# The first layer norm of the mixers, taken for whole sequences in the experts' preparation

## The chip, the cores and the metric

The kernel runs on one core of a Trainium2 chip. A core has five engines that run their own instruction streams and wait for each other by semaphores: TensorE (PE in the profile, with PEld for its weight loads), VectorE (DVE), ScalarE (ACT), GpSimd (POOL) and SyncE (SP), which here issues nearly all DMAs. The metric is the time of one execution on the device in microseconds, less being better. A profiled execution gives a span, from the first to the last instruction, and a trace of every instruction.

## What is computed

The input is 16 sequences of 512 tokens with 128 features, in float32. Two blocks follow one another, each of the form x + mixer(norm(x)) * silu(experts(norm(x))):

```python
xn = _layernorm(x)
s = _L0_attn_ref(xn, ...)        # four layers, see below
g = _silu(_L0_ffn_ref(xn, ...))  # 8 experts, 2 chosen for each token
x = x + s * g
xn = _layernorm(x)
s = _L1_attn_ref(xn, ...)        # windowed attention, 16 heads of 64
g = _silu(_L1_ffn_ref(xn, ...))  # 32 experts, 4 chosen, and a shared one
x = x + s * g

def _layer(x, p):                # one of the four layers of _L0_attn_ref
    x = x + _attention(_layernorm(x, ln1w, ln1b), aw, ab, pw, pb)
    h = _layernorm(x, ln2w, ln2b)
    return x + gelu(h @ fw + fb) @ mw + mb
```

The mixer's `_attention` has no scores. It makes q, k and v, turns each into quaternions (the value, its difference to the token before, a rolled copy, a cosine), multiplies them pointwise, applies a fixed spectral filter and projects. Tokens meet only in the difference to the token before. Each of the four layers has two norms over the features, so each sequence needs eight. The change concerns the first of these eight.

## The kernel before

Features lie on the 128 partitions and tokens along the free axis, so a whole sequence is a tile of 128x512 and half a sequence one of 128x256. The program has two stages. The first does the mixer, both sets of experts and the routing; the second is the windowed attention and the last sum, and the change does not touch it.

**Mixers.** Four mixer streams p = 0 to 3 run through the first stage (`mixer_stream`, L532): streams 0 and 2 take the even sequences, 1 and 3 the odd ones; streams 0 and 1 take the first half of a sequence (h0) and 2 and 3 the second (h1). A name such as `f4h1l0a` is sequence 4, second half, layer 0, first norm; `b` is the second norm. Each stream has its own PSUM bank (m0 to m3), its own tile `big` and its own tile `normed[p]` of 128x256. The layer (`mixer_layer`, L427) is written as a Python generator: each `yield` ends a step, and a layer has ten: two for the first norm, then qkv, the cosines, the quaternion products, filter and projection, two for the second norm, the Gelu part and the last product. Four layers and one step for the output make `STEPS_M` = 41 steps for a sequence.

**A norm** (`norm`, L176) subtracts no mean here, because the mixer's data are in a basis where the mean is one component. It squares on ACT (L185), sums over the partitions by products with a column on PE into `pv` (L189, 128 tokens at a time), copies with an epsilon on ACT into `ve` (L198), takes the power -1/2 on POOL into `rs` (L200), spreads that over the partitions by products on PE into `bc` (L203), and multiplies on DVE (L213 for the mixers, L211 for the experts' norms, which subtract the mean first and call their tiles sq and xs).

**Experts.** The expert work is one sequence of jobs, called the feed. `prep0` (L246) prepares a sequence for the first experts: it loads x, norms it, turns it into the mixers' basis (the product `pz` on PE, the copy to the tile `z` on ACT, L258), hands z to the mixers through `given[b]`, computes the router's logits `pl`, chooses experts and writes the gates to DRAM. `loop0` (L284) then runs the eight experts, in 16 chunks: products `pg` (L299) and `pu` (L301), Silu (L303), a product on DVE (L304), the summing product `acc` (L305). `prep1` (L380) and `loop1` (L395) do the same for the second experts (L405 to L419); prep1 needs both halves of the first block's output for its sequence. The preparation of the next job is interleaved with the loop of the present one. All preparations share one PSUM bank, "b", the loops have one bank each for pg, pu and acc, and the tiles tagged "h" (three buffers) serve both the chunks of the loops and the norms of the preparations.

**The order.** A loop at the end of the stage calls the streams in turn, stream p starting `LAG * p` turns late (LAG = 5), and after each call advances the feed by a rate worked out from `STEPS_M`, so that a pair of sequences in the mixers meets its share of expert steps (9 per sequence of loop0, 18 of loop1). This gives the program order. Mixer steps are given a priority 400 instructions ahead of their place; from priorities and its own estimate of times a scheduler then makes the fixed instruction order of each engine. The engines run their orders strictly in turn, so an instruction that waits holds up all behind it on its engine.

**The first norm** of layer 0 is done in `mixer_layer` like any other: each stream norms its half of z into `normed[p]`, and the products of q, k and v (L443) read it. The same tile takes the other seven norms of the stream.

Of the kernel before, what the change touches and what calls it, by code (L numbers as in the profile page):

```python
# [10 lines left out]
F32 = mybir.dt.float32  # L11
# [4 lines left out]
P = 128  # L16
NB = 16
S = 512
# [12 lines left out]

TWO_PI_BELOW = 6.283185

STEPS_M, STEPS_0, STEPS_1 = 41, 9, 18

LAG = 5

# [18 lines left out]
def recurrent_kernel(ctx: ExitStack, tc: tile.TileContext, a, out):  # L56
    nc = tc.nc

    const = ctx.enter_context(tc.tile_pool(name="const", bufs=1))
# [14 lines left out]
    for l in range(L):  # L74
        t = wl.tile([P, W_END, P], F32, tag="lw", name=f"lw{l}")
# [20 lines left out]
    filt = cst[:, C_G : C_G + S]  # L96
# [23 lines left out]
    nc.gpsimd.memset(quarter, 0.25)  # L120

    normed = [const.tile([P, T], F32, name=f"normed{p}") for p in range(4)]
    for t in normed:
        nc.gpsimd.memset(t, 1.0)

    def fold(l, pa, pc, pool):
# [49 lines left out]
    def norm(src, dst, sq, bank, name, xs=None, p="e"):  # L176


        if xs is not None:
            xc = bank(f"xc_{name}")  # L180
            nc.tensor.matmul(xc, lhsT=centre, rhs=src, start=True, stop=True)
            nc.scalar.activation(sq, xc, AF.Square)
            nc.scalar.copy(xs, xc)
        else:
            nc.scalar.activation(sq, src, AF.Square)  # L185
        pv = bank(f"pv_{name}")
        n = src.shape[-1] // P
        for k in range(n):
            nc.tensor.matmul(  # L189
                pv[:, k : k + 1],  # L190
                lhsT=sq[:, k * P : (k + 1) * P],
                rhs=mean_col if xs is not None else mean_col0,
                start=True,
                stop=True,
            )
        yield
        ve = small.tile([P, NBLK], F32, tag=f"ve{p}", name=f"ve_{name}", bufs=2)
        nc.scalar.activation(ve[:, :n], pv[:, :n], AF.Identity, bias=eps)  # L198
        rs = small.tile([P, NBLK], F32, tag=f"rs{p}", name=f"rs_{name}", bufs=2)
        nc.gpsimd.tensor_tensor(rs[:, :n], in0=ve[:, :n], in1=nhalf[:, :n], op=ALU.pow)  # L200
        bc = bank(f"bc_{name}")
        for k in range(n):
            nc.tensor.matmul(  # L203
                bc[:, k * P : (k + 1) * P],
                lhsT=rs[:, k : k + 1].to_broadcast([P, P]),
                rhs=ident,
                start=True,
                stop=True,
            )
        if xs is not None:  # L210
            nc.vector.tensor_mul(dst, bc[:, : n * P], xs)  # L211
        else:
            nc.vector.tensor_mul(dst[: P - 1], bc[: P - 1, : n * P], src[: P - 1])  # L213
        yield
# [8 lines left out]
    def top_k(mask, n, k, name):  # L223

        best = small.tile([P, NBLK, 8], F32, tag="best", name=f"best_{name}", bufs=2)
        hit = small.tile([P, NBLK, n + 8 - k], F32, tag=f"hit{n}", name=f"hit_{name}", bufs=1)
        for i in range(NBLK):
            nc.vector.max(out=best[:, i, :], in_=chosen[n][:, i, :n])
        nc.vector.memset(best[:, :, k:], LOW)
        for i in range(NBLK):  # L230
            nc.vector.match_replace(
                out=hit[:, i, :], in_to_replace=best[:, i, :], in_values=chosen[n][:, i, :], imm_value=HIT
            )
        nc.vector.tensor_scalar(mask, hit[:, :, :n], HIT, None, ALU.is_equal)

    def to_rows(gates, n, gd, pool, bank, name):

        pg = bank(f"pt_{name}")
        for k in range(NBLK):
            nc.tensor.transpose(pg[:n, k * P : (k + 1) * P], gates[:, k, :], ident)  # L240
        gt = pool.tile([n, S], F32, tag=f"gt{n}", name=f"gt_{name}", bufs=1)
        nc.scalar.copy(gt, pg[:n, :])
        nc.sync.dma_start(gd, gt)


    def prep0(b, pool, ps, given, kept):  # L246

        name = f"e{b}"
        x = pool.tile([P, S], F32, tag="x", name=f"x_{name}", bufs=2)
        nc.sync.dma_start(x, a["xT"][:, b * S : (b + 1) * S])  # L250
        xn = pool.tile([P, S], F32, tag="xn", name=f"xn_{name}", bufs=2)
        sq = pool.tile([P, S], F32, tag="h", name=f"sq_{name}", bufs=3)
        xs = pool.tile([P, S], F32, tag="h", name=f"xs_{name}", bufs=3)
        yield from norm(x, xn, sq, ps["b"], name, xs)
        pz = ps["b"](f"pz_{name}")
        nc.tensor.matmul(pz, lhsT=basis, rhs=xn, start=True, stop=True)
        z = pool.tile([P, S], F32, tag="z", name=f"z_{name}", bufs=4)
        nc.scalar.copy(z, pz)  # L258
        last = small.tile([P, L, 3], F32, tag="last", name=f"last_{name}", bufs=6)
        given[b] = [z, None, last]  # L260
        pl = ps["b"](f"pl_{name}")
        for k in range(NBLK):
            nc.tensor.matmul(
                pl[:, k * NE0 : (k + 1) * NE0], lhsT=xn[:, k * P : (k + 1) * P], rhs=rw0, start=True, stop=True
            )
        plv = pl[:, : NBLK * NE0].rearrange("p (k e) -> p k e", e=NE0)
        work = chosen[NE0][:, :, :NE0]
        nc.vector.tensor_copy(work, plv)
        sg = small.tile([P, NBLK, NE0], F32, tag="sg0", name=f"sg_{name}", bufs=1)
        nc.scalar.activation(sg, work, AF.Sigmoid)  # L270
        mask = small.tile([P, NBLK, NE0], F32, tag="mk0", name=f"mk_{name}", bufs=1)
        top_k(mask, NE0, K0, f"{name}tk")
        yield
        nc.vector.tensor_mul(sg, sg, mask)
        den = small.tile([P, NBLK], F32, tag="den", name=f"den_{name}")
        nc.vector.tensor_reduce(den, sg, axis=AX.X, op=ALU.add)
        nc.vector.tensor_scalar_add(den, den, 1e-10)
        nc.vector.reciprocal(den, den)
        nc.vector.tensor_tensor(sg, sg, den.unsqueeze(2).to_broadcast([P, NBLK, NE0]), op=ALU.mult)
        to_rows(sg, NE0, gd0[b], pool, ps["b"], name)  # L280
        yield
        kept[0, b] = xn
# [141 lines left out]
        yield  # L424


    def mixer_layer(l, s, big, A, filt, last, bank, pool, name, p):  # L427


        first, last = last  # L430
# [2 lines left out]

        qkv = big.rearrange("p (i c) t -> p i c t", c=4)

        sq, h, z = big[:, 1, :], normed[p], big[:, 0, :]
        yield from norm(s, h, sq, bank, f"{name}a", p=p)
        raw, steps, turns = qkv[:, :, 0, :], qkv[:, :, 1, :], qkv[:, :, 3, :]
        for at in (slice(0, 2), slice(2, 3)):
            pq = bank(f"pq{at.start}_{name}")[:, : (at.stop - at.start) * T]  # L440
# [11 lines left out]
        for i, n in ((0, 2), (2, 1)):  # L452
            at = slice(i, i + n)
# [55 lines left out]
            s1, in0=po, scalar=turned[:, l, 0:1], in1=s, op0=ALU.add, op1=ALU.add  # L509
        )  # L510
        yield
        yield from norm(s1, h, sq, bank, f"{name}b", p=p)
        hid = A
        for i in range(0, 4, 2):
# [17 lines left out]
    def mixer_stream(seqs, half, pool, bank, p, given, written):  # L532

        at = slice(half * T, (half + 1) * T)
        for b in seqs:
            name = f"f{b}h{half}"
            while b not in given:
                yield
            z, _, last = given[b]
            s = z[:, at]  # L540
            for l in range(L):
                big = pool.tile([P, 12, T], F32, tag=f"big{p}", name=f"big_{name}l{l}")
                A = pool.tile([P, 4, T], F32, tag=f"A{p}", name=f"A_{name}l{l}")
                s = yield from mixer_layer(
                    l, s, big, A, filt[:, at], (half == 0, last[:, l, :]), bank, pool, f"{name}l{l}", p
                )
            while given[b][1] is None:
                yield
            x = pool.tile([P, T], F32, tag=f"xe{p}", name=f"x_{name}", bufs=1)
            nc.sync.dma_start(x, a["xT"][:, b * S + half * T : b * S + (half + 1) * T])  # L550
            g0 = given[b][1][:, at]
            pn = bank(f"pn_{name}")[:, :T]
            nc.tensor.matmul(pn, lhsT=basis, rhs=s, start=True, stop=True)
            nc.vector.tensor_mul(g0, pn, g0)
            nc.gpsimd.tensor_add(x, x, g0)
            nc.sync.dma_start(x1[b][:, at], x)
            written[b] += 1
            yield

    with (  # L560
# [3 lines left out]
        def banks(tag, n=1, width=S):  # L564
            return lambda name: psum.tile([P, width], F32, tag=tag, name=name, bufs=n)

        ps = {t: banks(t, n) for t, n in (("b", 1), ("g", 1), ("u", 1), ("acc", 1))}
# [53 lines left out]
    for i in range(2):  # L621
        t = wl.tile([P, NCH // 2, B_END, P], F32, tag="lw", name=f"aw{i}")
# [18 lines left out]
    with (  # L641
# [3 lines left out]
        ps = {  # L645
            tag: (lambda name, tag=tag, n=n: psum.tile([P, S], F32, tag=tag, name=name, bufs=n))
            for tag, n in (("pa", 2), ("ps", 2), ("pt", 2), ("po", 1), ("acc", 1))
        }
# [298 lines left out]
```

## Time and profile before

| | |
|---|---|
| median of 3 timed runs | 4145.51 us (4137.9 to 4149.45) |
| profiled execution, its own time | 4143.72 us |
| its span | 4141.9 us |
| mean granted TensorE clock | 0.979 |
| PE, DVE busy over the span | 3884.2 us (94%), 3465.7 us (84%) |
| ACT, POOL busy over the span | 2503.8 us (60%), 1626.7 us (39%) |
| first product of the attention stage | 2936 us |

The page divides the span into 40 slices of some 103 us and prints the busy share of each in tenths, 9 being 90% or more:

```profile
PE   8899989999999999899999999898999999999999
DVE  5788898989989898999888998985677777777776
ACT  3556665566565566556656565552477766767776
POOL 1122232222222223222222222220477777777776
```

The first 28 or so slices are the first stage, and the change of pattern on POOL marks the attention. Busy time is a mean over stages with different limits, so what a change is worth has to be read in its own stage. Matmuls are pipelined, and a busy PE in this profile is not PE at its peak. "Idle before" in a group's row is the time the engine stood still just ahead of these instructions, followed by what ended it; idle time of an engine that is not the limit costs nothing.

### The profile page before, as it was taken

To read this page: it belongs to the slowest core of one execution; us is meant where nothing else is said; L and a number is where in the kernel's file an instruction comes from. 1 tells how busy PE (TensorE), PEld (TensorE's weight loads), DVE (VectorE), ACT (ScalarE), POOL (GpSimd) and SP (SyncE) were. 2 spreads that over 40 slices of the span, in tenths; PEclk is the share of its full clock that TensorE was granted. 3 is DMA by queue.
4 is the path that set the end of the run, shared out by engine and by line. 5 is a ranking of instruction groups with operands and counts; after the bars stand their busy time and mean duration, and the time that the engine had idled before them with its cause. 6 is when DMAs were issued, how large, how long until landed. Compare 5 with 4: busy or idle time off the path is not lost. (4 is left out here: it accounts for less than half of the span.)

```text
span 4141.9 us, 56811 instructions
## 1 busy us (share of the span) xinstructions
PE 3884.2 (94%) x16936; PEld 2340.9 (57%) x16936; DVE 3465.7 (84%) x8220; ACT 2503.8 (60%) x5572; POOL 1626.7 (39%) x1885
## 2 busy tenths in 40 slices
PE   8899989999999999899999999898999999999999
PEld 5556655565555556566655655554455555555555
DVE  5788898989989898999888998985677777777776
ACT  3556665566565566556656565552477766767776
POOL 1122232222222223222222222220477777777776
PEclk8999999999999999999999999998999999999999
DMA  3222323322332332333233233243200000000000
GB/s 106 76 85 86 95 67 106 118 89 92 110 102 86 111 112 81 100 113 102 79 109 115 75 111 100 90 124 116 78 11 19 14 19 14 11 19 14 16 6 6
DMA packets 205972, 308.96 MB, mean 75 GB/s; under 512 B 29664, under 2 KB 121952, under 8 KB 205536
## 3 DMA queue, kind: packets, MB, share of 16 engines
q1 hardware_dynamic: 205520, 304.28, 24.1%
q8 instruction: 135, 2.21, 0.2%
q14 instruction: 173, 1.42, 0.1%
q10 hardware_dynamic: 144, 1.05, 0.1%
HBM read 236.79 MB, written 18.09 MB: 62 GB/s over the span
## 5 line engine op out<-in xcount | busy, mean ns | idle before, releaser
L405 PE MATMUL pg_m<-xn_m,w_m 128*128 128x512 f32 x544 | 294.4, 624 | 47.8 <-DMA w_m<-in_ew 40.7
L409 ACT ACTIVATE h_m<-pg_m 128x512 f32<-128x512 f32 x272 | 162.3, 597 | 278.2 <-PE pg_m L405 189.4
L407 PE MATMUL pu_m<-xn_m,w_m 128*128 128x512 f32 x544 | 288.7, 613 | 10.1 <-DVE h_m L410 9.9
L419 PE MATMUL acc_m<-h_m,w_m 128*128 128x512 f32 x544 | 284.6, 607 | 6.4 <-DVE h_m L418 5.8
L305 PE MATMUL acc_e<-h_e,w_e 128*128 128x512 f32 x512 | 270.2, 610 | 20.6 <-DVE h_e L304 20.2
L299 PE MATMUL pg_e<-xn_e,w_e 128*128 128x512 f32 x512 | 273.1, 615 | 16.2 <-ACT h_e L303 13.8
L301 PE MATMUL pu_e<-xg_e,w_e 128*128 128x512 f32 x512 | 265.0, 599 | 0.0
L410 DVE TENSOR_TENSOR h_m<-pu_m,h_m 128x512 f32<-128x512 f32 x272 | 185.6, 682 | 92.8 <-PE pu_m L407 69.1
L520 ACT ACT_TABLE_LOAD x203 | 260.4, 1283 | 3.6
L303 ACT ACTIVATE h_e<-pg_e 128x512 f32<-128x512 f32 x256 | 152.6, 596 | 181.5 <-PE acc_e L305 108.8
L304 DVE TENSOR_TENSOR h_e<-pu_e,h_e 128x512 f32<-128x512 f32 x256 | 174.6, 682 | 72.0 <-PE pu_e L301 67.7
L673 POOL TENSOR_TENSOR t_q<-t_q,rtab 128x512 f32<-128x512 f32 x128 | 162.6, 1271 | 91.3 <-DMA g_a<-g 88.8
L418 DVE TENSOR_TENSOR h_m<-gb_m,h_m 128x512 f32<-128x512 f32 x256 | 182.6, 713 | 16.1 <-DMA gb_m<-gd 14.9
L301 PEld LDWEIGHTS pu_e<-xg_e,w_e 128*128 128x128 f32 x512 | 98.5, 193 | 123.6 <-issue 123.6
L405 PEld LDWEIGHTS pg_m<-xn_m,w_m 128*128 128x128 f32 x544 | 95.4, 193 | 124.1 <-issue 74.3
L674 POOL TENSOR_TENSOR q<-q,t_q 128x512 f32<-128x512 f32 x128 | 163.1, 1274 | 0.1
L673 POOL TENSOR_TENSOR t_k<-t_k,rtab 128x512 f32<-128x512 f32 x128 | 162.6, 1270 | 0.9 <-DVE t_k L671 0.9
L674 POOL TENSOR_TENSOR k<-k,t_k 128x512 f32<-128x512 f32 x128 | 162.6, 1270 | 0.2
L685 PE MATMUL pv<-wv,xn_a 128*128 128x512 f32 x256 | 143.6, 644 | 11.2 <-DVE q L672 11.1
L407 PEld LDWEIGHTS pu_m<-xn_m,w_m 128*128 128x128 f32 x544 | 100.5, 195 | 89.7 <-issue 52.8
L668 PE MATMUL pa_q<-xn_a,aw 128*128 128x512 f32 x256 | 144.9, 648 | 5.3 <-DMA xn_a<-xn 5.3
L419 PEld LDWEIGHTS acc_m<-h_m,w_m 128*128 128x128 f32 x544 | 99.6, 192 | 81.2 <-issue 46.0
(6272 smaller groups left out, 11195.6 us busy)
## 6 DMA issues: line engine op xcount, KB each, us to landing
gb_m<-gd SPq DMA_DIRECT2D x512, 128.0 KB
w_m<-in_ew SPq DMA_DIRECT2D x272, 192.0 KB
w_e<-in_ew SPq DMA_DIRECT2D x128, 384.0 KB
gb_e<-gd SPq DMA_DIRECT2D x128, 256.0 KB
x_e<-in_xT SPq DMA_DIRECT2D x16, 256.0 KB
x_m<-x SPq DMA_DIRECT2D x16, 256.0 KB
xn<-xn_m SPq DMA_DIRECT2D x16, 256.0 KB
g<-g_m SPq DMA_DIRECT2D x16, 256.0 KB
```

Of the source, the lines that this page charges most:

```text
L299: nc.tensor.matmul(pg, lhsT=w[:, c, :], rhs=xn, start=True, stop=True)
L301: nc.tensor.matmul(pu, lhsT=w[:, 2 + c, :], rhs=xg, start=True, stop=True)
L304: nc.vector.tensor_mul(h, pu, h)
L305: nc.tensor.matmul(acc, lhsT=w[:, 4 + c, :], rhs=h, start=(e == 0 and c == 0), stop=(e == NE0 - 1 and c == HID0 // P - 1),)
L405: nc.tensor.matmul(pg, lhsT=w[:, 0, :], rhs=xn, start=True, stop=True)
L407: nc.tensor.matmul(pu, lhsT=w[:, 1, :], rhs=xn, start=True, stop=True)
L410: nc.vector.tensor_mul(h, pu, h)
L418: nc.vector.tensor_mul(h, gb, h)
L419: nc.tensor.matmul(acc, lhsT=w[:, 2, :], rhs=h, start=(c == 0), stop=shared)
L520: nc.scalar.activation(hid[:, i : i + 2, :], pf.rearrange("p (j t) -> p j t", t=T), AF.Gelu)
L673: nc.gpsimd.tensor_mul(t, t, rtab[:, 2 * which + 1, :])
L674: nc.gpsimd.tensor_add(dst, dst, t)
```

## The change

The first norm of layer 0 is taken out of the mixers and done in `prep0`, right behind the copy to z and before `given[b]` is set. It is done once for the sequence of 512 tokens instead of twice for 256. Its result goes to one of four new tiles `arrived` of 128x512, chosen by the sequence's number modulo 4, which the products of q, k and v of layer 0 read in halves. The new Square writes to a tile `sz` with the tag "h", and the sums and spread rows go through bank "b". The mixers' layer 0 has two steps less, and `STEPS_M` becomes 39. The other seven norms stay.

```diff
-STEPS_M, STEPS_0, STEPS_1 = 41, 9, 18
+STEPS_M, STEPS_0, STEPS_1 = 39, 9, 18
...
     normed = [const.tile([P, T], F32, name=f"normed{p}") for p in range(4)]
-    for t in normed:
+
+    arrived = [const.tile([P, S], F32, name=f"arrived{i}") for i in range(4)]
+    for t in normed + arrived:
         nc.gpsimd.memset(t, 1.0)
...
         nc.scalar.copy(z, pz)
         last = small.tile([P, L, 3], F32, tag="last", name=f"last_{name}", bufs=6)
+        sq = pool.tile([P, S], F32, tag="h", name=f"sz_{name}", bufs=3)
+        yield from norm(z, arrived[b % 4], sq, ps["b"], f"{name}z")
         given[b] = [z, None, last]
...
-    def mixer_layer(l, s, big, A, filt, last, bank, pool, name, p):
+    def mixer_layer(l, s, h0, big, A, filt, last, bank, pool, name, p):
...
-        sq, h, z = big[:, 1, :], normed[p], big[:, 0, :]
-        yield from norm(s, h, sq, bank, f"{name}a", p=p)
+        sq, h, z = big[:, 1, :], h0, big[:, 0, :]
+        if l:
+            h = normed[p]
+            yield from norm(s, h, sq, bank, f"{name}a", p=p)
...
+        h = normed[p]
         yield from norm(s1, h, sq, bank, f"{name}b", p=p)
...
                 s = yield from mixer_layer(
-                    l, s, big, A, filt[:, at], (half == 0, last[:, l, :]), bank, pool, f"{name}l{l}", p
+                    l, s, arrived[b % 4][:, at], big, A, filt[:, at], (half == 0, last[:, l, :]), bank, pool, f"{name}l{l}", p
                 )
```

## The prediction

> **What bounds the kernel now.** I read the page's digit rows first, to cut the span, then busy time by stage. One execution takes 4141.9 us of span, 4143.72 us with what lies around it; the three timed runs have a median of 4145.51 us, 1.8 us more. I sum against 4143.7.
>
> The busy times by stage (start:end, length, then PE, PEld, DVE, ACT, POOL busy, TensorE clock, DMA share, GB/s), steady part, end of the first stage, attention stage:
>
> ```profile
> 100.00:2850.00 2750.00, 2544.98 (x9526) 1595.72 (x9525) 2434.14 (x4400) 1612.64 (x2669) 718.57 (x817) 0.98 0.32 97
> 2791.50:2936.00 144.50, 121.26 (x310) 57.78 (x310) 72.77 (x163) 39.39 (x63) 6.82 (x9) 0.89 0.39 118
> 2936.00:4142.00 1206.00, 1180.12 (x6912) 655.20 (x6912) 933.74 (x3600) 840.02 (x2817) 896.11 (x1040) 1.00 0.05 16
> ```
>
> The change touches nothing in the third row; its 1206 us stay. In the first, PE is busy 93%, DVE 89%, ACT 59%, POOL 26%: two engines near full, and no single wait to pull out. As a busy PE includes pipelined overlap, I also took its pace from the starts of matmuls: a 512-column pass follows the last after 0.43 us, 256 after 0.215, 128 or fewer after 0.11. By these pitches the first stage is 2531 us of PE work in 2936 us. Between 100 and 2850 us the starts lie 361 us wider than that: 85 us ended on ACT, 60 on DVE, 50 on POOL (all at the broadcast products bc), 63 on a DMA or DMA with ACT, 84 at no wait (mostly the clock of 0.98). So the stage is paced by PE in a fixed order with small hiccups, and the change can only shift the hiccups.
>
> The groups of ACT (line, operation, tiles | busy, mean ns | idle before, who ended it):
>
> ```profile
> L520 ACT ACT_TABLE_LOAD x201 | 257.9, 1283 | 3.6
> L303 ACT ACTIVATE h_e<-pg_e 128x512 f32<-128x512 f32 x251 | 149.6, 596 | 173.3 <-PE acc_e L305 108.8 <-PE pg_e L299 51.3 <-PE acc_m L419 4.9
> L303 ACT ACT_TABLE_LOAD x102 | 130.9, 1283 | 7.2 <-PE pv_e L189 3.5 <-PE pv_m L189 1.3 <-DVE xn_m L211 0.6
> L409 ACT ACT_TABLE_LOAD x99 | 127.0, 1283 | 5.5 <-PE pv_m L189 3.8
> ```
>
> Two things to see: most of ACT's big rows are table switches, and the expert's Silu waits 108.8 us for acc_e, that is for one of the three buffers "h" to come free.
>
> One removed norm in order of time (start, length, engine, line), the first half of sequence 4:
>
> ```profile
> 697.58 0.50 PE L189 MATMUL pv_f4h0l0a<-cst,big_f4h0l 128*128 128x1 f32 x4
> 698.27 0.26 ACT L198 ACTIVATE ve_f4h0l0a<-pv_f4h0l0a,eps 128x2 f32<-128x2 f32 x1
> ...
> 698.61 0.83 POOL L200 TENSOR_TENSOR rs_f4h0l0a<-ve_f4h0l0a,nhalf 128x2 f32<-128x2 f32 x1 [0.59 <-ACT ve_f4h0l0a L198]
> ...
> 702.33 0.61 PE L203 MATMUL bc_f4h0l0a<-cst,rs_f4h0l0a 128*128 128x128 f32 x4
> ...
> 703.81 0.41 DVE L213 TENSOR_TENSOR normed<-bc_f4h0l0a,z_e 127x256 f32<-127x256 f32 x1
> ```
>
> It takes 6.6 us from pv to the product's end, but PE does other work from 698.1 to 702.3: the chain is hidden behind experts.
>
> **The change part by part.**
>
> *Work.* Removed, 32 times: Square 0.416, ve 0.258, rs about 0.70, product 0.424 us. Added, 16 times at 512 columns, by the rows of the expert norm: Square 0.597, ve 0.258, rs 1.03, product 0.682. ACT 21.6 - 13.7 = -7.9 us, DVE 13.6 - 10.9 = -2.7, POOL 22.4 - 16.5 = -6. PE nothing: four passes more or less either way (16x8 pv and bc passes for 32x4). None of this is on PE, so I cost it at nothing.
>
> *PE's waits at the norm.* Ahead of the 32 removed bc the starts show 5.4 us of hiccup, ahead of their pv 2.1. The nearest row for what comes is the expert norm in the same preparation: 1.2 and 1.4 us for 16. **-5 us** (from -7.5, no new wait, to +5, if each new norm waits as the router's norm does: 5.6 + 2.4 us there).
>
> *Table loads.* The instruction order shows 476 loads before and 416 after (Gelu 203 to 175, expert Silu 105 to 85, router-expert Silu 100 to 91). At 1283 ns that is 77 us of ACT. The Trainium skill, ScalarE: Activation LUTs, "What ACT_TABLE_LOAD costs", counts a drain of about 1380 ns on top, 2.66 us a switch: 160 us. The trace disagrees: a load at 1713.64 us ended at 1714.92 and the Silu began at 1714.94. I take 1283. But ACT idles 41% of the stage, so only what reaches PE counts: 85 us over 476 loads is 0.18 us a load, times 60 is **-11 us**. Ends: 0 (none on the path) and -43 (half of all that ended on ACT).
>
> *The new Square's buffer.* sz is taken from the three "h" that the expert loop rotates through. Its hold, from Square to last pv, is 4.4 us in the mean for sq_e. What that costs is in no row; near it is the hold of sq_e and xs_e together, 12.5 us, in which PE's hiccups are 16.8% against 14.0% overall (0.35 us each); for the router norm 22.3% of 14 us (1.15 us). **+6 us** for 16; ends 0 and +35 (PE loses half of 16 x 4.4).
>
> *What is queued behind.* In the preparation the router's logits now come after the new norm, since all use the one PSUM bank "b": the chain grows by about 12.5 us, as long as the first norm. The gates are written 22 us or more before the loop that needs them (sequences 4 and 5 the closest), apart from sequence 0; so at nothing, and 16 x a few us if that lead were gone. On ACT, Silus queue behind the new Square and ve; on POOL the mixers' differences behind rs, which waited 60.6 us for ve_e in its ten waits. A norm issues no DMA; SP only sees the layer-0 swaps earlier. The first pair has no lead: z of sequence 1 is used 4 us after it is made. But in the new order the first products of sequence 1 stand at the same place in PE's queue (row 104 in both), and half 1 of sequence 0 comes before the weight folding instead of amid it: nothing. The memsets of arrived, 4 x some 0.6 us (a 256-column one is 0.31), end before POOL's first rs (22 us).
>
> *Fewer steps.* Mixers go from 41 to 39 turns, and expert steps per turn rise to match. PE work is unchanged, so at a full PE this is worth nothing in itself; it moves the end of the stage.
>
> *The end of the stage.* Rows of PE in order of time:
>
> ```profile
> 2791.52 1.06 PE L181 MATMUL xc_m<-x_m,cst 128*128 128x512 f32 x2
> ...
> 2801.73 1.92 PE L323 MATMUL pl_m<-rw,xn_m 128*128 128x32 f32 x8 [3.25 <-DVE xn_m L211]
> 2803.46 2.05 PE L405 MATMUL pg_m<-xn_m,w_m 128*128 128x512 f32 x2
> ...
> 2827.60 3.09 PE L419 MATMUL acc_m<-h_m,w_m 128*128 128x512 f32 x4 [0.26 <-DVE h_m L418]
> ...
> 2837.83 1.02 PE L419 MATMUL acc_m<-h_m,w_m 128*128 128x512 f32 x2
> 2843.86 2.08 PE L181 MATMUL xc_m<-x_m,cst 128*128 128x512 f32 x2 [5.00 <-DMA x_m<-x]
> ```
>
> From the norm of sequence 14 (2791.5) to attention (2936) are 144.5 us for 104.2 us of PE work: 40 lost, part of it behind sequence 15, whose mixer ended late (the 5.00 us). In the new order the last mixer ends 105 us of PE work ahead of attention instead of 83, and the norm of 14 begins with 95.7 left and no mixer beside it. Its chain to the first acc (36 us here) then holds 11.7 us of work: 24 lost, the 5.00 us gone, 5 lost at attention's first load as now, some 5 for the cold clock: 34. That is 130 us, plus 8.5 us more work ahead of it at 0.88: 140. **-5 us**, ends -10 and +8. The skill's TensorE: Matmul & The Clock Gate, "What's actually happening", speaks against this step: after an idle window of some 3.4 us the array runs at half clock until it has been busy as long. The trace agrees (pairs 1.7 to 1.8 us apart at 2803 to 2811, 0.86 later), so a bare chain is paid twice. By the rule alone two cold windows would lose about 2 x 3.4/2 = 3.4 us; I took 5.
>
> *The redrawn order.* The scheduler re-sorts everything. PE work between a mixer's pv and its bc has a median of 3.4 us before and 3.0 after (68 of 256 under 2.5, then 77 of 226); between an expert's pu and acc, and Gelu and pm, the same. I cost it at nothing, +-15.
>
> Sum: -5 - 11 + 6 - 5 = -15 us: 4143.7 to **4129**, against the median 4145.5 about **4130 us**, 0.37% less.
>
> **Rivals.** *ACT is the true pace* (for: table loads are its largest rows; against: 41% idle, 85 us of PE's hiccups in all). The -11 becomes -43: 4097 us. Chance 0.08.
>
> *The h ring.* Place: L303's wait for acc_e. A slot lent to sz stops one chunk in three just when the ring is the limit, and the norm now sits in the expert's own order, no longer in the mixers' preferred one. Price: 16 x 4.4 us, half lost, +35 for the +6: about 4159 us; all lost, +70: 4194. It decides from 1.3 us per preparation, where it eats the 21 us of gains. For: 108.8 us of waits at that place. Against: the present two borrowers cost 0.35 us. Chance 0.26.
>
> *It moves nothing*: the norm was hidden before, table loads go from idle time, the end of the stage comes out even: 4144 us. For: ACT's 41%, the hidden chain above. Against: the 5.00 us. Chance 0.14.
>
> That the change does not do what it says is excluded: the norms l0a are gone from the order and 16 of 512 columns stand in it.
>
> **The numbers.** Forecast 0.52, by itself 4110 to 4148. A measurement here tells 0.3% (12 us) from no change. Faster: 0.36 of the forecast and the first rival's 0.08, 0.44. Same: 0.15 of the forecast, 0.11 of the third and 0.02 of the ring, 0.28. Slower: 0.24 of the ring, the rest of the others, 0.28. The range runs from the first rival's time to 4172, a little beyond the ring's half price.
>
> **What would show it.** ACT's loads at 416 and its busy time down by 80 to 90 us; PE's busy time unchanged; PE's hiccups ended on ACT near 75 us and on POOL below 50; ahead of the last x_m no wait; a bare stretch of some 20 us on PE behind the norm of sequence 14. The ring is right if L303's wait for acc_e grows by 20 us or more and PE waits at sz's pv. I am wrong altogether if the steady stage from 100 to 2700 us differs by over 1% at the same work: then the new order's own waits decide.

## The result, and the profile after

| | before | changed |
|---|---|---|
| median, lowest to highest | 4146.33 us (4137.9 to 4149.45, 4 runs) | 4164.18 us (4159.08 to 4166.02, 4 runs) |
| profiled execution, its span | 4143.72, 4141.9 us | 4163.71, 4161.9 us |
| mean granted clock | 0.979 | 0.978 |
| ACT busy, instructions | 2503.8 us, 5572 | 2422.5 us, 5480 |

The changed kernel takes 1.0044 [1.0027, 1.0062] of the time before: some 18 us more, where 16 less were forecast. The direction is wrong. That the time lies in the forecast's range is luck: the range reached up to 4172 us for the sake of the h ring, which is not what happened (below).

The same stages of the changed kernel (columns as in the prediction's first view; the first product of attention is now 17 us later, at 2953 us):

```profile
100.00:2850.00 2750.00, 2535.24 (x9472) 1590.60 (x9470) 2415.58 (x4372) 1525.87 (x2566) 720.78 (x796) 0.97 0.32 96
2950.00:4162.00 1212.00, 1182.56 (x6912) 656.32 (x6912) 934.79 (x3600) 840.17 (x2817) 896.40 (x1040) 1.00 0.05 16
```

In the first row ACT has 87 us less to do and PE has done *less* in the same 2750 us, 9472 matmuls for 9526. Attention is as it was. Two shorter stretches show where PE falls behind; first before, then changed:

```profile
100.00:400.00 300.00, 277.37 (x1005) 168.75 (x1004) 247.79 (x440) 170.99 (x287) 74.78 (x84) 0.97 0.27 83
400.00:2500.00 2100.00, 1963.27 (x7433) 1237.03 (x7432) 1901.77 (x3437) 1268.50 (x2092) 563.81 (x640) 0.99 0.33 99
```

```profile
100.00:400.00 300.00, 284.08 (x1084) 178.52 (x1083) 261.94 (x463) 173.07 (x294) 79.83 (x87) 0.98 0.28 84
400.00:2500.00 2100.00, 1943.89 (x7327) 1225.79 (x7326) 1873.62 (x3378) 1174.44 (x1987) 568.76 (x627) 0.98 0.33 96
```

Up to 400 us the changed kernel is ahead: 1084 matmuls for 1005. From 400 to 2500 us it makes 7327 where before makes 7433, 1.4% less on a stage that PE paces.

Equal times hold unequal work. So I gave each matmul of a trace the pitch that the prediction found for its width, summed these pitches to "PE work", and asked how much longer than its PE work each stretch *of work* took. A "hiccup" is the time by which the next matmul starts later than the pitch. The first stage is 2531 us of PE work in both kernels. The time over that, in one profiled execution of each:

| PE work, us | 0 to 300 (start) | 300 to 2200 (steady) | 2200 to 2531 (end) |
|---|---|---|---|
| before | 74 us | 229 us | 93 us |
| changed | 54 us | 271 us | 90 us |
| difference | -20 | +42 | -3 |

These make nearly all of the 20 us between the two profiled executions. By what ended PE's hiccups in the steady part, the 42 us are spread: DMA, alone or with ACT, 56 to 71; POOL 34 to 44; no wait shown 52 to 62 (the granted clock over this part is 0.986 before and 0.981 changed); DVE 34 to 42; ACT 55 to 52. No single wait carries them. How a hiccup with two causes is sorted matters: by the one releaser that the profile names, ACT goes from 54 to 61 and DMA from 47 to 55. Only the spread is firm.

The groups of ACT that the prediction showed, now, between 100 and 2850 us (L527, L307 and L413 are its L520, L303 and L409):

```profile
L527 ACT ACT_TABLE_LOAD x173 | 222.0, 1283 | 3.1
L307 ACT ACTIVATE h_e<-pg_e 128x512 f32<-128x512 f32 x250 | 149.1, 596 | 204.8 <-PE acc_e L309 110.0 <-PE pg_e L303 71.2 <-PE acc_m L423 5.1
L413 ACT ACT_TABLE_LOAD x90 | 115.5, 1283 | 3.0 <-PE pv_e L191 1.3 <-PE pv_m L191 0.2
L307 ACT ACT_TABLE_LOAD x83 | 106.5, 1283 | 9.2 <-PE pv_e4z L191 3.2 <-PE pv_e L191 2.6 <-PE pv_m L191 1.3
```

The loads went as forecast. The wait for acc_e, where the h ring would show, stands at 110.0 us for 108.8. PE's waits in the same window moved at places that no edit touches, the second experts' among them (line, waited for: us in total, times, longest); before, then changed:

```profile
PE pg_m L405 <- DMA w_m<-in_ew: 39.0, 39, 3.9
PE pg_m L405 <- ACT h_m L409: 5.3, 8, 1.4
```

```profile
PE pg_m L409 <- DMA w_m<-in_ew: 41.2, 38, 3.2
PE pg_m L409 <- ACT h_m L413: 14.5, 13, 2.5
...
PE bc_e5z L205 <- POOL rs_e5z L202: 3.5, 1, 3.5
```

The new norm has one noticeable wait, the last row; it was once late, not sixteen times.

### The profile page after: what moved, and what is told of

Same layout as the page of the kernel before. It is cut to its first block, busy times and chain, and to the rows that moved or that the text cites. A ratio compares the mean times of both kernels' runs of the same rounds, so it can differ in the third digit from the quotient of the medians.

```text
span 4161.9 us, 56676 instructions
## 1 busy us (share of the span) xinstructions
PE 3887.7 (93%) x16936; PEld 2340.1 (56%) x16936; DVE 3457.6 (83%) x8204; ACT 2422.5 (58%) x5480; POOL 1634.9 (39%) x1873
## 5 line engine op out<-in xcount | busy, mean ns | idle before, releaser
L413 ACT ACTIVATE h_m<-pg_m 128x512 f32<-128x512 f32 x272 | 162.4, 597 | 328.7 <-PE pg_m L409 223.5
L409 PE MATMUL pg_m<-xn_m,w_m 128*128 128x512 f32 x544 | 296.3, 627 | 61.1 <-DMA w_m<-in_ew 44.2
L303 PE MATMUL pg_e<-xn_e,w_e 128*128 128x512 f32 x512 | 269.3, 608 | 17.0 <-ACT h_e L307 10.9
L307 ACT ACTIVATE h_e<-pg_e 128x512 f32<-128x512 f32 x256 | 152.7, 596 | 209.1 <-PE acc_e L309 110.0
L409 PEld LDWEIGHTS pg_m<-xn_m,w_m 128*128 128x128 f32 x544 | 95.6, 195 | 143.8 <-issue 78.8
```

Source lines behind the costliest of these rows:

```text
L303: nc.tensor.matmul(pg, lhsT=w[:, c, :], rhs=xn, start=True, stop=True)
L409: nc.tensor.matmul(pg, lhsT=w[:, 0, :], rhs=xn, start=True, stop=True)
```

## The experiments

Every ratio is to the kernel before, run on the same chip, with its 95% interval. "Steady" is the middle column of the table above, and "start" and "end" are its neighbours; each is from one profiled execution, which lay up to 13 us from its kernel's median. Steady compares with 229 before and 271 changed. In the expectations, the "order theory" says that any new instruction order costs, and the "place" or "move" theory that the norm costs by standing in the preparation.

### The ring, the steps, the order: one part at a time

**A buffer of its own for sz.**

```diff
-        sq = pool.tile([P, S], F32, tag="h", name=f"sz_{name}", bufs=3)
+        sq = pool.tile([P, S], F32, tag="sz", name=f"sz_{name}", bufs=1)
```

> The changed kernel, with the new Square's tile sz in a buffer of its own instead of one of the three h that the expert loops rotate through. The h ring theory: most of the 18 us comes back, about 4148 us, and PE's hiccups in the steady stage fall. The order theory (the scheduler's new order is what costs, whichever edit draws it): the time has no reason to return; 4140 to 4175, since this edit redraws the order once more (table loads 484 instead of 416).

4178.4 us, 1.0085 [1.0071, 1.0098]; steady 262. Freed from the ring, the kernel is slower still. ACT's row for the first experts' Silu:

```profile
L307 ACT ACTIVATE h_e<-pg_e 128x512 f32<-128x512 f32 x251 | 149.6, 596 | 174.0 <-PE acc_e L309 93.2 <-PE pg_e L303 71.2 <-PE acc_m L423 4.6
```

The wait for acc_e fell from 110.0 to 93.2 us and the time rose by 14. As this edit redraws the order too, the run alone can't exclude a small price of the ring. But in the changed kernel's trace sz is held for 2.9 us in the mean, 16 times, and PE's hiccups in these stretches are 2.6% of the time. The ring as the cause falls.

**The changed kernel with 41 steps**: two empty steps in layer 0 in place of the removed ones.

```diff
-STEPS_M, STEPS_0, STEPS_1 = 39, 9, 18
+STEPS_M, STEPS_0, STEPS_1 = 41, 9, 18
...
+        else:
+            yield
+            yield
```

> The changed kernel with two empty steps in layer 0 where the norm was, so that a sequence takes 41 turns of the mixers again and the expert steps per turn are those of before. If the shorter count of steps (39) is what costs, it returns to about 4146. If the bunching of the streams costs (two or three streams finish a sequence within 30 us of PE work of each other, instead of evenly spread), it stays at 4155 or more, because its streams end at 0, 78, 98 and 106 us of PE work for sequences 8 and 9 (before: 0, 34, 65, 104; changed: 0, 68, 97, 103).

4159.67 us, 1.0035 [1.0022, 1.0048]; steady 257.

**The kernel before with 39 steps**: all norms as before, but that of layer 0 ends no step.

```diff
-STEPS_M, STEPS_0, STEPS_1 = 41, 9, 18
+STEPS_M, STEPS_0, STEPS_1 = 39, 9, 18
...
-        yield from norm(s, h, sq, bank, f"{name}a", p=p)
+        for _ in norm(s, h, sq, bank, f"{name}a", p=p):
+            if l:
+                yield
```

> The kernel before with the norm left in the mixers, in halves, but without its two steps in layer 0, so 39 turns. Only the step count changes. If the step count costs: about 4164, as the changed kernel. If what costs is where the norm stands (bank b, h, the experts' order): about 4146. The order theory: anything from 4135 to 4170; its streams end at 0, 61, 100, 111 and it loads 507 tables.

4179.66 us, 1.009 [1.0077, 1.0103]; steady 270, and slower than any of the times expected. The step count alone, with the same instructions on every engine but the table loads, costs 0.9%; given back to the changed kernel, it brings about 4.5 us, hardly more than the intervals. So it is no fixed price of two steps. It is a new order, and a new order can cost more than the whole change.

**The changed kernel, mixers 500 ahead.**

```diff
-AHEAD = 400
+AHEAD = 500
```

> The changed kernel with the mixers' priority 500 instructions ahead instead of 400; the same instructions in another order. Its streams end evenly spread, at 0, 44, 74 and 97 us of PE work for sequences 8 and 9, like before. The bunching theory: 4146 or less. The theory that the norm's new place itself costs (h ring, bank b): about 4164 as the changed kernel. The last mixer ends 152 us of PE work ahead of the attention (changed kernel: 105), which can cost some us at the stage's end under either.

4164.54 us, 1.0054 [1.004, 1.0068]; steady 260. The streams end evenly spread and nothing came back, so the bunching theory falls.

### Both kernels at other settings of the order

If any redrawing costs time, the kernel before must lose too when only the settings change. LAG is the delay between streams, AHEAD the mixers' priority; each edit is one number. First LAG 4 and AHEAD 300, in both kernels:

> The kernel before with LAG 4 instead of 5: the same instructions in another order, norm in the mixers. The order theory: before's own order is the odd one, so this is slower too, by 10 to 40 us (4153 to 4185). The theory that the norm's move itself costs in the steady stage: within some us of before, 4135 to 4155.

> The changed kernel with LAG 4. Its pair is e5. The order theory: as e5 or, by the start that became 15 to 20 us shorter with the norm in the preparation, 5 to 20 us below e5. The move theory: 15 to 20 us above e5. By the distances in PE's order alone (pv to bc under 2.5 us for 20% of the norms, 34% in the changed kernel) it would be the better of the changed orders: 4145 to 4155.

> The kernel before with the mixers' priority 300 instructions ahead. Again the same instructions in another order; its streams end bunched, at 0, 87, 123 and 125 us of PE work. The order theory: 4153 to 4185. The bunching theory: slow, 4160 or more. The move theory: 4135 to 4155.

> The changed kernel with 300 instructions ahead, the pair of e7; bunched as well (0, 84, 113, 122). The order theory: at e7 or up to 20 us below it. The move theory: 15 to 20 us above e7.

Then LAG 6 in both, and AHEAD 500 in the kernel before:

> The kernel before with LAG 6: the third neighbouring setting of it. If its setting of 5 and 400 is a chosen low point, 10 to 40 us above it (4152 to 4182), as LAG 4 (4172.6) was. Its streams end evenly spread (0, 22, 56, 95).

> The changed kernel with LAG 6, pair of e9. If the change by itself gains (20 us in the first 300 us of PE work, in every changed kernel so far but e1) and only the steady stage is redrawn, it ends below e9 as with LAG 4 (-18) and 300 ahead (-102). If the norm in the preparation costs in the steady stage by itself (+31 at LAG 4, +42 at LAG 5), it ends 10 to 25 above e9.

> The kernel before with 500 instructions ahead; the order changes little (streams end at 0, 40, 63, 103; table loads 497). Within 10 us of before (4135 to 4155) if nearness of the order is what keeps the time. Its pair is e4 (4164.5).

| LAG, AHEAD | before | changed | changed less before, from the ratios | from the profiles: start, steady, end |
|---|---|---|---|---|
| 5, 400 | 4146.33 us, 1 | 4164.18 us, 1.0044 [1.0027, 1.0062] | +18 us | -20, +42, -3 |
| 4, 400 | 4172.61 us, 1.0080 [1.0065, 1.0095] | 4154.49 us, 1.0037 [1.0024, 1.0049] | -18 us | -38, +32, -28 |
| 5, 500 | 4161.78 us, 1.0045 [1.0029, 1.0061] | 4164.54 us, 1.0054 [1.0040, 1.0068] | +4 us | -5, +15, -9 |
| 6, 400 | 4181.69 us, 1.0083 [1.0068, 1.0099] | 4191.82 us, 1.0116 [1.0099, 1.0132] | +14 us | -7, +55, -19 |
| 5, 300 | 4276.34 us, 1.0326 [1.0310, 1.0342] | 4174.72 us, 1.0088 [1.0072, 1.0103] | -99 us | -25, -47, -21 |

The left column holds the same work five times: 4146 to 4276 us, the present setting its lowest point. The changed kernel spans 4154 to 4192, and its best is elsewhere, at LAG 4. The sign of the change depends on the setting. An edit that redraws the order can give up a setting that was the best of its own family.

The last column shows more than scatter. At all five settings the changed kernel gains at the start and at the end, and at four of them it loses in the steady part. Nor does every redrawing cost in the steady part: the kernel before with LAG 4 is better there than with LAG 5 (214 for 229) and loses at the start (92 for 74) and at the end (134 for 93).

Three expectations missed here. The kernel before with 500 ahead was to stay within 10 us and took some 19 more; with 300 ahead it was to stay within 4185 us; and the changed kernel with 300 ahead was to end at most 20 us below that, and ended 99 below. That a near order keeps the time falls with the first.

The settings show something of the table loads too. The pages' first rows (busy us, share, instructions) of the kernel before with AHEAD 300, then of the changed one with LAG 4:

```profile
PE 3914.1 (92%) x16936; PEld 2344.4 (55%) x16936; DVE 3467.8 (81%) x8220; ACT 2457.7 (58%) x5538; POOL 1626.3 (38%) x1885
```

```profile
PE 3878.2 (93%) x16936; PEld 2343.4 (56%) x16936; DVE 3464.7 (83%) x8204; ACT 2494.3 (60%) x5539; POOL 1652.9 (40%) x1873
```

ACT's instructions other than loads are 5572 - 476 = 5096 before and 5480 - 416 = 5064 changed. So the slowest kernel here has only 442 loads, 34 fewer than the original, and the changed one at its best has 475, 59 more than at the present setting. The 60 loads saved belong to one order, not to the change, and the time doesn't follow their number.

### The size, the place and the shape of the moved norm

**Moved for sequences 0 and 1 only.** The others are normed in the mixers as before; 41 steps.

```diff
-        sq = pool.tile([P, S], F32, tag="h", name=f"sz_{name}", bufs=3)
-        yield from norm(z, arrived[b % 4], sq, ps["b"], f"{name}z")
+        if b < 2:
+            sq = pool.tile([P, S], F32, tag="h", name=f"sz_{name}", bufs=3)
+            yield from norm(z, arrived[b], sq, ps["b"], f"{name}z")
...
```

> The norm taken in the preparation for sequences 0 and 1 alone, 41 steps for all; the others norm in the mixers as before. The start's gain of 20 us should appear whole, so at 300 us of PE work the loss is near 62 us (before: 83). If the steady stage costs because the norm stands in the preparation, its steady loss is as before (229) and the time is about 4125. If any redrawn order costs there, 250 to 275 and the time is 4140 to 4170.

4143.89 us, 0.9995 [0.9985, 1.0005]. Its profiled execution was 10 us above its median, so its split (59, 255, 91) says only that the start was short again. Whether the start can be gained alone was tried once more, with AHEAD 450:

> The kernel of e12 (norm moved for sequences 0 and 1 only) with 450 instructions ahead. The start's gain of 15 us stays; the steady loss is a new draw, 215 to 275 by what the others showed: 4125 to 4170, most likely 4150.

4178.09 us, 1.0074 [1.0058, 1.009], start 75. The gain at the start was expected to stay and did not: moving the norm of the first pair alone does not secure it.

**The moved norm four times over**, with its two steps ended only behind the last.

```diff
-        sq = pool.tile([P, S], F32, tag="h", name=f"sz_{name}", bufs=3)
-        yield from norm(z, arrived[b % 4], sq, ps["b"], f"{name}z")
+        for i in range(4):
+            sq = pool.tile([P, S], F32, tag="h", name=f"sz{i}_{name}", bufs=3)
+            for _ in norm(z, arrived[b % 4], sq, ps["b"], f"{name}z{i}"):
+                pass
+        yield
+        yield
```

> The changed kernel with the moved norm done four times over in the preparation (the result of the last is used). PE gets 3 x 16 x 1.75 = 84 us more work. The order theory: 4164 + 84, +-25, so 4223 to 4273. The place theory (each norm in the preparation costs some 40/16 = 2.5 us of hiccups in the steady stage beyond its own work): 3 x 42 more, so 4360 or above.

4238.3 us, 1.0223 [1.0202, 1.0244]: 74 us over the changed kernel for 83 us more PE work (2614 for 2531 by the same pitches). Forty-eight more of these norms, each with its Square, its hold of the ring and its place in bank "b", cost no more than their passes on PE, as far as one draw of the order can tell. No hidden price shows that grows with the number of norms.

**The moved norm with the mixers' priority.**

```diff
-        sq = pool.tile([P, S], F32, tag="h", name=f"sz_{name}", bufs=3)
-        yield from norm(z, arrived[b % 4], sq, ps["b"], f"{name}z")
+        with tc.high_priority(offset=AHEAD):
+            sq = pool.tile([P, S], F32, tag="h", name=f"sz_{name}", bufs=3)
+            for _ in norm(z, arrived[b % 4], sq, ps["b"], f"{name}z"):
+                pass
+        yield
+        yield
```

> The changed kernel, the moved norm with a priority 400 instructions ahead like the mixers' steps. If the low priority of the norm is what costs: steady loss near 229, time about 4125 to 4140. The order theory: no better than the others, 4150 to 4180.

4202.82 us, 1.0136 [1.0117, 1.0155]; steady 293, slower than either theory had it. That the norm came too late for want of priority falls.

**Whole sequences, but in the mixers.** Streams 0 and 1 norm the whole of z into `arrived`, in their own bank and with their own buffer and priority; streams 2 and 3 have two empty steps; 41 steps as before.

```diff
-STEPS_M, STEPS_0, STEPS_1 = 39, 9, 18
+STEPS_M, STEPS_0, STEPS_1 = 41, 9, 18
...
-        sq = pool.tile([P, S], F32, tag="h", name=f"sz_{name}", bufs=3)
-        yield from norm(z, arrived[b % 4], sq, ps["b"], f"{name}z")
...
+        elif p < 2:
+            z0, dst = whole
+            yield from norm(z0, dst, big[:, 2:4, :].rearrange("p a t -> p (a t)"), bank, f"{name}a", p=p)
+        else:
+            yield
+            yield
...
```

> Whole sequences and the tiles arrived as in the change, but done by streams 0 and 1 in their layer 0 with their own bank and buffer and the mixers' priority; 41 steps for all. The place theory: the steady loss (300 to 2200 us of PE work) falls from 271 to about 229. The order theory: 245 to 275 like the other redrawn ones, 4155 to 4180 in all.

4133.35 us, 0.9975 [0.996, 0.9989]: faster than both, steady 238. The order theory's 4155 to 4180 missed. The same at two more settings:

> e14 with LAG 4; there the kernel before took 4172.6 and the changed one 4154.5. If the place is what e14 gains by: 20 to 30 us below the changed one, 4125 to 4135. If e14 is a good draw: around the two, 4150 to 4175.

> e14 with 500 instructions ahead; there the kernel before took 4161.8 and the changed one 4164.5. If the place: 4130 to 4145. If a good draw: 4150 to 4170.

| LAG, AHEAD | whole sequences in the mixers | below before | below changed | steady: before, changed, this |
|---|---|---|---|---|
| 5, 400 | 4133.35 us, 0.9975 [0.9960, 0.9989] | 10 us | 29 us | 229, 271, 238 |
| 4, 400 | 4131.52 us, 0.9985 [0.9973, 0.9996] | 39 us | 22 us | 214, 246, 209 |
| 5, 500 | 4144.79 us, 1.0007 [1.0000, 1.0015] | 16 us | 19 us | 245, 260, 233 |

Both came out as the place theory had them. Over 2100 us in the steady part (columns as above), this kernel with LAG 5 and AHEAD 400:

```profile
400.00:2500.00 2100.00, 1957.89 (x7380) 1229.06 (x7379) 1876.18 (x3405) 1254.38 (x2054) 564.74 (x621) 0.98 0.33 99
```

With LAG 4, the changed kernel and then this one:

```profile
400.00:2500.00 2100.00, 1956.58 (x7351) 1230.50 (x7349) 1877.50 (x3396) 1250.94 (x2050) 569.32 (x622) 0.98 0.32 98
400.00:2500.00 2100.00, 1973.54 (x7450) 1240.07 (x7449) 1890.04 (x3427) 1266.40 (x2067) 563.82 (x625) 0.99 0.34 101
```

The work and the shape are the changed kernel's; the place differs, and the count of steps, 41 for 39. Steady loses 33, 37 and 27 us less, much alike where the orders' own scatter is wide. Against the changed kernel with 41 steps (257) it is 19 at the present setting, so the place is worth some 20 to 35 us of the steady part. In whole times the present setting gives a chain, from the ratios: whole sequences in the mixers -10 us, their move into the preparation (41 steps) +25, two steps less +4; together the +18. Each link is a new order too, and three settings are few.

Through which queue the preparation costs that isn't shown. Of the changed kernel's hiccups that end on a wait, only those ended on DVE exceed this kernel's at all three settings, by 5, 23 and 19 us. Bank "b" alone, the logits' later place alone and the two more steps of the preparation alone weren't tried.

## Why the prediction was wrong, point by point

**The redrawn order**, "at nothing, +-15", is the step that failed, and with it the norm's new place, which the prediction priced only through the h ring. The steady stage lost 42 us, where the prediction's terms for the waits and the table loads there made it shorter. Over the stretch for which the prediction named 1% as the sign that it was wrong altogether, 100 to 2700 us, the same work took 30 us or 1.2% longer. It looked for the cost at median distances of work between a product and its user. The share of short ones between a mixer's pv and bc did grow (27% to 34%; the changed kernel has 224 such norms, not the 226 of the prediction), but that does not decide: with 41 steps it is 26%, about that of before, and steady is still 257. The cost is in hiccups of all sizes at many places: of 41 us more, 18 are in hiccups under 1 us and 16 in those over 2 us. By the last table some 20 to 35 of the 42 us go with the place of the norm; the rest is the draw, and the runs don't divide them better than that. Why the place costs stays open.

The prediction also assumed that a redrawing is as likely to gain as to lose. For this kernel four redrawings of the same work, and a fifth with fewer steps, lost 15 to 130 us and none gained.

**"What is queued behind", "at nothing"**, was wrong the other way at the start: -20 us. PE is the better filled there (120 to 160 us; before, then changed):

```profile
120.00:160.00 40.00, 29.57 (x74) 13.92 (x73) 36.40 (x52) 18.78 (x32) 8.54 (x10) 0.92 0.28 87
```

```profile
120.00:160.00 40.00, 35.85 (x121) 19.54 (x120) 39.93 (x62) 19.18 (x38) 11.85 (x13) 1.00 0.37 113
```

The clock is 1.00 for 0.92 with it. The first expert product starts at 73.68 us where it started at 79.51. The start is shorter than that of before at all five settings, by 5 to 38 us. The order has a part in it: the unmoved norm with LAG 6 also has a start of 61, while the changed kernel with a buffer of its own for sz has 77.

**Table loads** were right on ACT and unproven on PE. 416 loads came and ACT's busy time fell by 81 us. PE's hiccups ended on ACT alone fell from 85 to 74, the 11 forecast, but those ended on DMA or on DMA with ACT rose from 63 to 81, and by the profile's own releaser ACT's share does not move (83 us in both). So the agreement is partly one of sorting. Those on POOL, forecast below 50, rose from 50 to 60; all together went from 361 to 376. And the saving is the order's, not the change's. The rival of ACT as the true pace falls with it.

**PE's waits at the norm**, forecast -5: 7.5 us went, 4.3 came at bc and none at pv, so -3. Right in size; the other mixer norms' bc gave it back, some 13 us more in all (second norm of layer 2 from 4.4 to 14.2 us, of layer 3 from 4.2 to 11.2; that of layer 1 fell).

**The h ring**, +6, and its rival: not seen. PE's hiccups while the expert norms hold their buffers went from 16.8% to 14.2% of the time, the wait for acc_e barely moved, and a buffer of its own for sz did not help.

**The end**, forecast -5: measured -3 (-9 to -28 at the other settings), much as the prediction had it. From the norm of sequence 14 to attention it took 126 us, forecast 130. PE's rows in order of time, changed:

```profile
2821.56 2.14 PE L423 MATMUL acc_m<-h_m,w_m 128*128 128x512 f32 x4
2827.33 2.07 PE L183 MATMUL xc_m<-x_m,cst 128*128 128x512 f32 x2 [3.63 <-DMA x_m<-x]
2830.57 1.87 PE L191 MATMUL pv_m<-cst,sq_m 128*128 128x1 f32 x8 [1.16 <-ACT xs_m L185]
2833.89 2.08 PE L205 MATMUL bc_m<-cst,rs_m 128*128 128x128 f32 x8 [1.45 <-POOL rs_m L202]
2836.82 1.91 PE L327 MATMUL pl_m<-rw,xn_m 128*128 128x32 f32 x8 [0.85 <-DVE xn_m L213]
2838.54 2.06 PE L409 MATMUL pg_m<-xn_m,w_m 128*128 128x512 f32 x2
```

The bare chain is there, from the last acc_m (2821.56) to the first pg_m (2838.54), and the half clock behind it: from 2838.5 to 2842.1 us the granted clock is 0.50, and the pair at 2838.54 is paced at 1.85 us, later ones at 0.86. (Before, too, the slow pairs behind the chain end at 2809 us and not, as the prediction read them, at 2811.) The wait for x_m did not vanish, though: before, 5.00 us stood ahead of the norm of sequence 15; now 3.63 stand ahead of that of 14.

**Fewer steps**, "nothing in itself": as a count of work right, as an order wrong. Alone it cost the kernel before 0.9%, and the changed kernel some 4 us.

## What to carry to other kernels

Where a scheduler fixes the order, an edit is the edit and a new draw: before judging one, run the kernel before and after at several settings of the order (here LAG and AHEAD) and compare families, stretch of work by stretch, since one pair can show +18 and the next -18 us. A saving on an engine that idles 40% is worth what PE's waits on it were, and the next late wait takes part of that; count it as zero until the sum of PE's hiccups falls. When an edit changes shape and place together, try the shape in the old place: here that version was the fastest, 4133 us with the present setting and 4132 with LAG 4.

## What was not expected of the hardware

The same instructions, the table loads aside, ran in 4146 or in 4276 us with only their order changed, by 130 us or 3%, at almost equal mean clocks of 0.979 and 0.974. And 77 us of table loads could leave ACT with at most 11 us of it reaching PE, while a kernel with 34 loads fewer than the original was the slowest of its family.
